# A graph-and-experts network on one core: sums products tied to later gathers in the edge layers, and records of four numbers in the first edge sort

## The chip, the cores and the metric

The kernel runs on one core of a Trainium2 chip. The metric is the device time of one execution in microseconds; lower is better. Five engines of the core matter: TensorE (PE in the profile, with its weight loads PEld), VectorE (DVE), ScalarE (ACT), GpSimd (POOL) and SyncE (SP), and the core's 16 DMA engines.

## The reference, cut to what matters

The network has 3125 nodes of 256 numbers and 53125 edges (src, dst), and four layers, each added to x: an attention over the edges, a mixture of 16 experts, a layer of typed relations over the edges, and a feed-forward of half the tokens.

```python
# layer 0, per head h of 4 (feats = LN(x) @ Ws[h] + bs[h], 64 wide)
score = a_s[:, src] + a_d[:, dst] + aw_e[:, None] * elem[None, :] + ab[:, None]
w = jnp.exp(-jax.nn.relu(score / 20.0))
pooled = segment_sum(w[:, None] * feats[:, dst], src)     # sums over the edges of a node
out = pooled / segment_sum(w, src)[..., None]
...
# layer 2 (called layer 1 of the edges here), h = LN(x)
score = h[src] @ w_src + h[dst] @ w_dst + rel_emb[etype] @ w_rel
alpha = exp(leaky_relu(score)); alpha /= sum(alpha, axis=1)   # one number per edge
msg = (h[src] + rel_emb[etype]) @ weight_neighbor * alpha
node = relu(segment_sum(msg, dst)) + where(in_deg > 0, h @ loop_weight, h @ evolve_loop_weight)
```

The edges are given in the order of dst. Layer 0 sums by src, so its edges are sorted by src in the kernel; layer 1 sums by dst and takes them as they come. `elem` (edge_weight) is float32 and must keep its 32 bits through the sort.

## The kernel before

**Order of the program.** `run` (L2047) goes through: the sort of layer 0's edges with the features of layer 0 between its steps; edge layer 0 (`heads_edges`, L1055) with two fillers, the layout of layer 1's edges and the gate of the experts, which is called for the bucket just finished and has its larger part after every fifth bucket; the experts; the router; edge layer 1 (`relations_edges`, L1621); the last feed-forward (`depths`). A second use of `sort_edges` for layer 1 stands under a branch that is taken only where the edges do not come in order.

**The sort** (`sort_edges`, L297). The edges lie as 128 x 416. `load_in` (L321) packs each into V small numbers that float16 holds exactly (`dig`): the other node's number less an offset, the row in its bucket of 128 nodes (plus 1, so that 0 means an empty place), and, with `bits`, the float32 weight as three pieces of 11, 11 and 10 bits. V is 5 with the weight and 3 without. `places` computes where each edge goes. `move` (L564) runs 13 times, over 32 columns each: for eight columns at a time, DVE compares (`hp`, `hk`) and spreads the records over the places (`hv`, four instructions of 128x400 at L593), and TensorE multiplies the two at L598, adding up in one bank of PSUM. ScalarE copies the result (L606) and GpSimd scatters it with five indirect DMAs (L609) into the table `s_tab` in DRAM, one row of eight records per partition. `load` (L618) reads the table back when all 65 scatters have landed, turns it with TensorE, and unpacks `idx`, `row` and `val` with DVE; `join_bits` (L787) puts the three pieces together. The first gather of edge layer 0 needs `idx`.

**An edge layer.** The edges lie in 25 buckets of 128 nodes, 24 of 18 tiles and one of 8, a tile being 128 edges: 440 tiles. Six tiles are a group; a bucket is three groups. `edge_stages` (L874) gives three stages and `pipelined` (L966) interleaves them: at step s it issues gather(s), message(s-1) and add(s-2), in this order on each engine.

- gather: six indirect DMAs of GpSimd (L907), one per tile, each fetching 128 table rows into one of `deep` buffers `rows` (5 in layer 0, 4 in layer 1); DVE builds the one-hot matrices `oh` (L915) and `hot` (L924).
- message: `near` products of TensorE (L933), reduced by DVE (L940), then `messages`: weights per edge by DVE and ScalarE. In layer 0 the rows are multiplied in place (L1099); in layer 1 ScalarE scales the one-hots (`ohw`, L1645) and the rows get a one-hot of the relation. Before a bucket's second group in layer 1, `loops` (L1650) computes the node's own part into PSUM (L1654), where `finish` of the bucket before must have read its own.
- add: TensorE sums the messages into the bucket's nodes (L953), one float32 product per tile, 260 columns wide in layer 0 and 457 in layer 1; the profile records each as two matmuls. When the bucket's last group is done, DVE adds the overflow (L961) and `finish` follows; in layer 1 that is two transposes at L1666 (`ps_cnt`), two products (`ps_rel`) and DVE's additions into x.

A buffer `rows` is free again when the add of its group is done; so gather(g) waits for add(g - deep). Within TensorE's order in layer 1, the first product of a new bucket stands between the two `ps_cnt` transposes of the bucket before, and its second to fifth before the products at L1654. Each indirect DMA signals one of eight completion semaphores, taken in turn, and a product waits for that of its own tile.

Of the kernel before, what the change touches and what calls it, by code (L numbers as in the profile page):

```python
# [9 lines left out]
F32 = mybir.dt.float32  # L10
BF16 = mybir.dt.bfloat16
F16 = mybir.dt.float16
I32 = mybir.dt.int32
AF = mybir.ActivationFunctionType
OP = mybir.AluOpType
AX = mybir.AxisListType
# [2 lines left out]
P = 128  # L19
# [3 lines left out]
class _Kernel:  # L23
# [8 lines left out]

    def __init__(self, ctx, tc, a, out):
        self.ctx, self.tc, self.nc, self.a, self.out = ctx, tc, tc.nc, a, out
# [259 lines left out]
    def sort_edges(self, pool, rp, name, seg, other, value, bits, tab, help, roomy, into=()):  # L297
# [23 lines left out]
        def load_in():  # L321
            seg_i = tmp(I32, "seg")
            self.load_edges(seg_i, seg, self.NP, nc.vector)
            oth_i = tmp(I32, "oth")
            self.load_edges(oth_i, other, 0, nc.vector)
            val = tmp(F32 if bits else I32, "val")
            self.load_edges(val, value, 0, nc.vector)
            yield
            vi = val.bitcast(I32) if bits else val
            bi = tmp(I32)  # L330
            nc.vector.tensor_scalar(bi, seg_i, 7, None, op0=OP.logical_shift_right)
            bf = tl([P, EC], F32, "bf")
            nc.vector.tensor_copy(bf, bi)
            st.update(bf=bf)
            if roomy:
                st["bt"] = tl([P, C, NS], BF16, "bt")
                nc.vector.tensor_copy(st["bt"], bi.rearrange("p (s t) -> p t s", t=C))


            dig = tl([P, V, EC], F16, "dig", pool)  # L340
            part = tmp(I32)
            nc.vector.tensor_scalar(part, seg_i, P - 1, None, op0=OP.bitwise_and)
            nc.vector.tensor_scalar(dig[:, 1, :], part, 1.0, None, op0=OP.add)
            nc.vector.tensor_scalar(dig[:, 0, :], oth_i, -float(self.half), None, op0=OP.add)
            if bits:
                for i, (sh, m) in enumerate(((0, 2047), (11, 2047), (22, 1023))):
                    v = tmp(I32)
                    nc.vector.tensor_scalar(
                        v, vi, sh, m, op0=OP.logical_shift_right, op1=OP.bitwise_and
                    )  # L350
                    nc.scalar.copy(dig[:, 2 + i, :], v)
            else:
                nc.scalar.copy(dig[:, 2, :], vi)
            st.update(dig=dig)
            yield
# [262 lines left out]
        def load():  # L618
            nb, m = self.KB, MT // self.KB
            if "idx" not in st:  # L620
                st.update(self.lists(name, 1 + (not bits)))
            wide = st["wide"]
            with tc.tile_pool(name=f"{name}_back", bufs=1) as bp:
                tk = bp.tile([P, nb, P, V], F16, name=f"{name}_tk")
                rows = tab[: MT * PT, :].rearrange("(k a) (e v) -> k (a e) v", a=PT, v=V)
                for i in range(nb):

                    queue = nc.gpsimd if roomy else nc.sync
                    ld = queue.dma_start(tk[:m, i], rows[i * m : (i + 1) * m])
                    for s in sent:  # L630
                        tc.add_manual_dep(
                            ld.ins, s.ins.name,
                            mybir.DependencyInfo(
                                mybir.DependencyClass.Sync, mybir.DependencyReason.DATA
                            ),
                            reason="sorted records",
                        )

                def turned(v):
                    pt = self.psum.tile([P, 1024], F16, tag="B", name=f"{name}_pt", bufs=4)  # L640
                    for i in range(nb):
# [11 lines left out]
                nc.vector.tensor_scalar(kept(st["row"]), turned(1), -1.0, None, op0=OP.add)  # L653
                for i, w in enumerate(wide):
                    wb = bp.tile([P, nb, P], BF16, name=f"{name}_wb{i}")
                    nc.vector.tensor_copy(wb[:m], tk[:m, :, :, 1 + i])
                    nc.sync.dma_start(w.rearrange("(i k) p -> k i p", k=m), wb[:m])
                if bits:
                    d = [bp.tile([P, MT], I32, name=f"{name}_d{v}") for v in range(3)]
                    for v in range(3):  # L660
                        nc.vector.tensor_copy(kept(d[v]), turned(2 + v))
                    self.join_bits(st["val"].bitcast(I32), d)
                else:
                    nc.vector.tensor_copy(kept(st["val"]), turned(2))
            return st

# [120 lines left out]
    def join_bits(self, out, d):  # L787
        nc = self.nc
        nc.vector.scalar_tensor_tensor(
            d[0], d[1], 11, d[0], op0=OP.logical_shift_left, op1=OP.bitwise_or  # L790
        )
        nc.vector.scalar_tensor_tensor(
            out, d[2], 22, d[0], op0=OP.logical_shift_left, op1=OP.bitwise_or
        )

# [11 lines left out]
    def edges_beyond(self, name, st, table, width, near, W, message, sums):  # L807
# [10 lines left out]
        with tc.If(more > 0):  # L818
            with tc.tile_pool(name=f"{name}_far", bufs=1) as pool:
# [6 lines left out]
                with tc.For_i(0, more) as k:  # L826
# [7 lines left out]
                    nc.vector.tensor_scalar(row, rec[:, 1:2], -1.0, None, op0=OP.add)  # L834
                    if V == 5:
                        d = tl("d", [3], I32)
                        nc.vector.tensor_copy(d, rec[:, 2:5])
                        self.join_bits(val.bitcast(I32), [d[:, i : i + 1] for i in range(3)])
                    else:
                        nc.vector.tensor_copy(val, rec[:, 2:3])  # L840
                    rows = tl("rows", [width])
                    nc.gpsimd.indirect_dma_start(
# [31 lines left out]
    def edge_stages(  # L874
# [27 lines left out]
        def gather(g, b, k, n, head, last):  # L902
            if head:
                now[b] = [spread(i, b) for i in range(len(st["wide"]))]
            rows = pool.tile([P, G, into], F32, name="rows", bufs=deep)
            for j in range(n):
                self.last_gather = nc.gpsimd.indirect_dma_start(  # L907
                    out=rows[:, j, :width], out_offset=None, in_=table,
                    in_offset=bass.IndirectOffsetOnAxis(
                        ap=st["idx"][:, k + j : k + j + 1], axis=0  # L910
                    ),
                )
            sh = [P, n, P]
            oh = pool.tile([P, G, P], F32, name="oh", bufs=3)
            nc.vector.tensor_tensor(  # L915
                oh[:, :n, :], numbers[:, None, :P].to_broadcast(sh),
                st["row"][:, k : k + n, None].to_broadcast(sh), op=OP.is_equal,
            )
# [29 lines left out]
        def add(g, b, k, n, head, last, oh, msg):  # L948
# [1 line left out]
                now["sum"] = sums2[:, b % 2 * 512 : (b % 2 + 1) * 512]  # L950
            ps = now["sum"]
            for j in range(n):
                nc.tensor.matmul(  # L953
                    ps[:, :W], oh[:, j, :], msg[:, j, :],
                    start=(head and j == 0), stop=(last and j == n - 1),
                )
            if last:
                more = pool.tile([P, W], F32, name="more")
                nc.sync.dma_start(more, sums[b])
                acc = pool.tile([P, W], F32, name="acc")  # L960
                nc.vector.tensor_add(acc, ps[:, :W], more)  # L961
                finish(b, acc)

        return gather, message, add

    def pipelined(self, stages, fill=()):  # L966

# [1079 lines left out]
    def run(self):  # L2047
# [110 lines left out]
```

## Time and profile before

| | us |
|---|---|
| median of 3 runs | 2326.38 (2322.57 to 2326.58) |
| the profiled execution | 2333.29 |
| its span | 2331.5 |
| mean granted clock of TensorE in it | 0.796 |

The stages, by where their instructions stand in the trace:

| stage | from to, us | what runs |
|---|---|---|
| packing, places | 0 to 109 | DVE, ScalarE |
| move and scatters of layer 0 | 109 to 268.5 | DVE, TensorE, 65 scatters |
| load, unpacking | 268.5 to 282 | DMA, DVE |
| edge layer 0 | 282 to 993 | gathers 282 to 968 |
| experts | 1045 to 1376 | TensorE |
| edge layer 1 | 1436 to 2190 | gathers 1436 to 2166 |
| last feed-forward | to 2331 | TensorE, DVE, DMA |

How the profile is read: the page has the busy time of each engine in 40 slices of the span, the groups of instructions by source line (busy time, mean duration of one in ns, and the idle time of the engine just before them with what ended it), and the waits. These are the 40 slices, busy share in tenths, with the clock that TensorE was granted:

```profile
PE   3787244343534544449999964677778777777588
DVE  8999444454444553553222244445556454554731
POOL 1088676656565664413333312455556555555051
PEclk7599666677666776659999987788888888888789
```

A slice is 58 us. The nines in DVE's second to fourth slice are the sort; PE's nines from slice 18 to 22 are the experts; the two long stretches of middling digits are the edge layers.

### The profile page before, as it was taken

How to read it: one execution, taken by the hardware profiler on the slowest of the kernel's cores; microseconds unless marked ns; L12 is line 12 of the kernel's file. 1: busy time of each engine (PE TensorE's matmuls, PEld its weight loads, DVE VectorE, ACT ScalarE, POOL GpSimd, SP SyncE). 2: the span in 40 equal slices, each digit the busy share in tenths (PEclk: the TensorE clock that was granted, in tenths of full speed). 3: DMA queues.
4: the chain of work that ended last, by engine and by line, in shares of the span. 5: the costliest groups of instructions: out<-in, count | busy, mean ns of one | idle time of the engine just before them, and what ended most of it. 6: DMA issues, size and time to landing. Idle time of an engine off the chain costs nothing. (4 is left out here: it accounts for less than half of the span.)

```text
span 2331.5 us, 22343 instructions
## 1 busy us (share of the span) xinstructions
PE 1514.6 (65%) x6602; PEld 940.0 (40%) x6602; DVE 1166.3 (50%) x3010; ACT 424.0 (18%) x1148; POOL 1127.2 (48%) x1133
## 2 busy tenths in 40 slices
PE   3787244343534544449999964677778777777588
PEld 1265133332433433326666643333334333333256
DVE  8999444454444553553222244445556454554731
ACT  1311000100001000102122224122222222222421
POOL 1088676656565664413333312455556555555051
PEclk7599666677666776659999987788888888888789
DMA  3040244443444443249999956444444444443130
GB/s 96 27 158 27 74 115 118 122 114 106 126 117 108 119 129 95 71 137 343 300 316 314 319 192 191 128 128 131 131 130 135 126 131 130 131 130 99 61 121 19
DMA packets 250714, 324.52 MB, mean 139 GB/s; under 512 B 38128, under 2 KB 185008, under 8 KB 250582
## 3 DMA queue, kind: packets, MB, share of 16 engines
q1 hardware_dynamic: 192214, 179.00, 24.6%
q0 software_dynamic: 51760, 137.35, 20.6%
q10 hardware_dynamic: 6608, 6.62, 0.8%
q8 instruction: 57, 0.93, 0.2%
q14 instruction: 75, 0.61, 0.1%
HBM read 286.26 MB, written 36.61 MB: 138 GB/s over the span
## 5 line engine op out<-in xcount | busy, mean ns | idle before, releaser
L907 POOL DMA_INDIRECT rows<-table,s_idx x880 | 836.8, 951 | 590.5 <-issue 291.7
L953 PE MATMUL ps_sums<-rows,oh 128*128 128x260 f32 x880 | 271.6, 474 | 250.0 <-issue 247.0
L953 PE MATMUL ps_sums<-rows,ohw 128*128 128x457 f32 x880 | 395.6, 597 | 13.6 <-issue 11.9
L953 PEld LDWEIGHTS ps_sums<-rows,oh 128*128 128x128 f32 x880 | 206.2, 241 | 302.2 <-issue 258.2
L953 PEld LDWEIGHTS ps_sums<-rows,ohw 128*128 128x128 f32 x880 | 177.4, 209 | 187.6 <-issue 169.7
L915 DVE TENSOR_TENSOR oh<-ps_hold,s_row 128x768 f32<-128x768 f32 (+1 forms) x148 | 139.2, 941 | 139.5 <-remote 103.6
L1387 PE MATMUL ps_h<-w,x_t 128*128 128x512 f32 x448 | 204.5, 599 | 0.0
L924 DVE TENSOR_SCALAR hot<-wide,pcols 128x768 bf16<-128x768 bf16 (+1 forms) x296 | 173.4, 591 | 26.7 <-remote 12.7
L1654 PE MATMUL ps_hold<-lw,x_t 128*128 128x512 f32 x100 | 82.8, 974 | 116.8 <-DVE oh L915 83.0
L1409 POOL DMA_INDIRECT ytab<-y,back x56 | 55.0, 982 | 203.2 <-DVE y L1408 194.3
L1645 ACT ACTIVATE ohw<-oh,s 128x128 f32<-128x128 f32 x440 | 136.3, 388 | 66.7 <-DVE s L1598 33.5
L940 DVE TENSOR_REDUCE near<-ps_near 128x24 f32<-128x72 f32 (+2 forms) x148 | 28.9, 197 | 236.8 <-remote 194.9
L1639 DVE TENSOR_TENSOR rows<-ps_hold,s_val 128x1200 f32<-128x1200 f32 x74 | 102.8, 1389 | 84.5 <-remote 34.2
L609 POOL DMA_INDIRECT s_tab<-s_rec,s_to x65 | 125.5, 1931 | 30.0 <-issue 18.8
L1393 DVE TENSOR_TENSOR hid<-hid,ps_h 128x512 f32<-128x512 f32 x56 | 38.5, 687 | 199.1 <-ACT hid L1392 195.4
L933 PEld LDWEIGHTS <-hot 128*128 128x128 bf16 x1760 | 64.6, 100 | 179.1 <-DVE hot L924 98.2
L1099 DVE TENSOR_TENSOR rows<-rows,ps_hold 128x1536 f32<-128x1536 f32 x74 | 128.0, 1730 | 0.7 <-ACT ps_hold L1097 0.3
L1387 PEld LDWEIGHTS ps_h<-w,x_t 128*128 128x128 f32 x448 | 81.7, 193 | 81.1 <-issue 81.0
L1404 PE MATMUL ps_y<-w,h_t 128*128 128x256 f32 x448 | 105.9, 379 | 0.7 <-ACT h_t L202 0.7
L1097 ACT ACTIVATE ps_hold<-s 128x24 f32<-128x24 f32 x74 | 14.3, 193 | 502.5 <-DVE s L1093 99.1
L961 DVE TENSOR_TENSOR acc<-ps_sums,more 128x260 f32<-128x260 f32 (+1 forms) x50 | 26.5, 529 | 155.9 <-remote 92.9
L593 DVE TENSOR_TENSOR s_hv<-s_hk,s_dig 128x400 f16<-128x400 f16 x208 | 100.6, 677 | 0.0
(410 smaller groups left out, 2057.4 us busy)
## 6 DMA issues: line engine op xcount, KB each, us to landing
w<-in_L_ffn_w_dram SPq DMA_DIRECT2D x168, 512.0 KB
wide<-s_w SPq DMA_DIRECT2D x72, 576.0 KB
rows<-table,s_idx POOLq DMA_INDIRECT x880
sums<-sums_z SPq DMA_DIRECT2D x5, 1142.5 KB
more<-sums SPq DMA_DIRECT2D x25, 228.5 KB
yg<-ytab SPq DMA_DIRECT2D x5, 1024.0 KB
sums<-sums_z SPq DMA_DIRECT2D x5, 650.0 KB
table<-f ACTq DMA_DIRECT2D x5, 650.0 KB
```

Of the source, the lines that this page charges most:

```text
L593: nc.vector.tensor_tensor(rec[:, i], hk[:, i, :, None, :].to_broadcast(sh), dig[:, None, :, t0 + 2 * i : t0 + 2 * i + 2].to_broadcast(sh), ...
L609: d = nc.gpsimd.indirect_dma_start(out=tab, out_offset=bass.IndirectOffsetOnAxis(ap=to[:, i : i + 1], axis=0), in_=out[:, k * CH * V : (k ...
L907: self.last_gather = nc.gpsimd.indirect_dma_start(out=rows[:, j, :width], out_offset=None, in_=table, in_offset=bass.IndirectOffsetOnAxis( ...
L915: nc.vector.tensor_tensor(oh[:, :n, :], numbers[:, None, :P].to_broadcast(sh), st["row"][:, k : k + n, None].to_broadcast(sh), op=OP.is_equal,
L924: nc.vector.tensor_scalar(t[:, : n // 2, :], w, at, None, op0=OP.is_equal)
L953: nc.tensor.matmul(ps[:, :W], oh[:, j, :], msg[:, j, :], start=(head and j == 0), stop=(last and j == n - 1),)
L1099: nc.vector.tensor_tensor(rows[:, :n, :HO].rearrange("p j (h o) -> p j h o", o=O), rows[:, :n, :HO].rearrange("p j (h o) -> p j h o", o=O) ...
L1387: nc.tensor.matmul(ph[:, i * HID : (i + 1) * HID], xt[:, c, :], w12[:, i, c, :], start=(c == 0), stop=(c == C - 1),)
L1404: nc.tensor.matmul(py[:, :D], ht[:, c, :], w3[:, c, :], start=(c == 0), stop=(c == HC - 1))
L1639: nc.vector.tensor_tensor(rows[:, :n, R0:], self.numbers[:, None, :R].to_broadcast(sh), st["val"][:, k : k + n, None].to_broadcast(sh), op ...
L1645: nc.scalar.activation(ow[:, j, :], oh[:, j, :], AF.Copy, scale=s[:, 1, j : j + 1])
L1654: nc.tensor.matmul(self.held_ps[:, : 2 * D], ht[:, c, :], lw[:, c].rearrange("p i d -> p (i d)"), start=(c == 0), stop=(c == C - 1),)
```

## The change

**Waits.** In gather, the six indirect DMAs are kept in a list; in add at the same step, which is two groups behind, each product takes the next of them and gets a dependence on it. Product j of group g thus waits for gather j of group g+2. Nothing else in the stages differs, and the order of instructions on each engine stays as it was. The last two groups have no gather to wait for.

**Records.** With the weight's bits, V is 4 instead of 5. The first number stays. The second holds the row and the weight's low four bits (16 times row plus bits, plus 1), up to 2048. The other 28 bits go as two numbers of 14, each plus 1024, written as the bit pattern of a float16. So `hv` is 128x320, a product of the sort 160 columns, a scattered row 64 bytes and the table a fifth smaller. Packing takes two more DVE operations, a ScalarE cast that also adds the 1 replaces three, and unpacking goes through `split_row` and two subtractions.

```diff
-            nc.vector.tensor_scalar(dig[:, 1, :], part, 1.0, None, op0=OP.add)
             if bits:
-                for i, (sh, m) in enumerate(((0, 2047), (11, 2047), (22, 1023))):
+                low = tmp(I32)
+                nc.vector.tensor_scalar(low, vi, 15, None, op0=OP.bitwise_and)
+                both = tmp(F32)
+                nc.vector.scalar_tensor_tensor(
+                    both, part, 16.0, low, op0=OP.mult, op1=OP.add
+                )
+                nc.scalar.activation(dig[:, 1, :], both, AF.Copy, bias=1.0)
+                for i, sh in enumerate((4, 18)):
                     v = tmp(I32)
                     nc.vector.tensor_scalar(
-                        v, vi, sh, m, op0=OP.logical_shift_right, op1=OP.bitwise_and
-                    )
-                    nc.scalar.copy(dig[:, 2 + i, :], v)
+                        v, vi, sh, 16383, op0=OP.logical_shift_right, op1=OP.bitwise_and
+                    )
+                    nc.vector.tensor_scalar(
+                        dig[:, 2 + i, :].bitcast(I16), v, float(self.LEAST), None, op0=OP.add
+                    )
...
                 if bits:
+                    self.split_row(
+                        bp.tile([P, nb, P], I32, name=f"{name}_wl")[:m],
+                        bp.tile([P, nb, P], I32, name=f"{name}_wh")[:m], tk[:m, :, :, 1],
+                        wb := bp.tile([P, nb, P], BF16, name=f"{name}_wb")[:m], 1.0,
+                    )
+                    nc.sync.dma_start(wide[0].rearrange("(i k) p -> k i p", k=m), wb)
                     d = [bp.tile([P, MT], I32, name=f"{name}_d{v}") for v in range(3)]
-                    for v in range(3):
-                        nc.vector.tensor_copy(kept(d[v]), turned(2 + v))
+                    self.split_row(kept(d[0]), kept(d[1]), turned(1), kept(st["row"]), 0.0)
+                    for v in (1, 2):
+                        nc.vector.tensor_scalar(
+                            kept(d[v]), turned(1 + v).bitcast(I16), float(self.LEAST), 0.0,
+                            op0=OP.subtract, op1=OP.max,
+                        )
                     self.join_bits(st["val"].bitcast(I32), d)
...
+    def split_row(self, low, high, src, row, add):
+        nc = self.nc
+        nc.vector.tensor_scalar(low, src, -1.0, None, op0=OP.add)
+        nc.vector.tensor_scalar(high, low, 4, None, op0=OP.arith_shift_right)
+        nc.vector.tensor_scalar(row, high, add, None, op0=OP.add)
+        nc.vector.tensor_scalar(low, low, 15, None, op0=OP.bitwise_and)
...
             rows = pool.tile([P, G, into], F32, name="rows", bufs=deep)
+            now["came"] = came = []
             for j in range(n):
                 self.last_gather = nc.gpsimd.indirect_dma_start(
...
+                came.append(self.last_gather)
...
             for j in range(n):
-                nc.tensor.matmul(
+                mm = nc.tensor.matmul(
                     ps[:, :W], oh[:, j, :], msg[:, j, :],
                     start=(head and j == 0), stop=(last and j == n - 1),
                 )
+                if now["came"]:
+                    self.behind(mm, now["came"].pop(0), "TensorE in step with the gathers")
...
+    def behind(self, ins, other, reason):
+        self.tc.add_manual_dep(
+            ins.ins, other.ins.name,
+            mybir.DependencyInfo(mybir.DependencyClass.Sync, mybir.DependencyReason.DATA),
+            reason=reason,
+        )
...
-        tab0, tab1 = self.edge_table("s0", 5), self.edge_table("s1", 3)
+        tab0, tab1 = self.edge_table("s0", 4), self.edge_table("s1", 3)
```

More of the change, by code (lines that the diff above doesn't have):

```diff
@@ L13 @@
 I32 = mybir.dt.int32
+I16 = mybir.dt.int16
 AF = mybir.ActivationFunctionType
@@ L23 @@
 class _Kernel:
+    LEAST = 1024
     def __init__(self, ctx, tc, a, out):
@@ L342, in load_in @@
             nc.vector.tensor_scalar(part, seg_i, P - 1, None, op0=OP.bitwise_and)
-            nc.vector.tensor_scalar(dig[:, 1, :], part, 1.0, None, op0=OP.add)
             nc.vector.tensor_scalar(dig[:, 0, :], oth_i, -float(self.half), None, op0=OP.add)
             if bits:
-                for i, (sh, m) in enumerate(((0, 2047), (11, 2047), (22, 1023))):
+                low = tmp(I32)
[6 more added lines that the diff above has]
+                for i, sh in enumerate((4, 18)):
                     v = tmp(I32)
                     nc.vector.tensor_scalar(
-                        v, vi, sh, m, op0=OP.logical_shift_right, op1=OP.bitwise_and
+                        v, vi, sh, 16383, op0=OP.logical_shift_right, op1=OP.bitwise_and
                     )
-                    nc.scalar.copy(dig[:, 2 + i, :], v)
+                    nc.vector.tensor_scalar(
+                        dig[:, 2 + i, :].bitcast(I16), v, float(self.LEAST), None, op0=OP.add
+                    )
             else:
+                nc.vector.tensor_scalar(dig[:, 1, :], part, 1.0, None, op0=OP.add)
                 nc.scalar.copy(dig[:, 2, :], vi)
@@ L652, in load @@
                 )
[L653 to L657, printed above, removed]
-                if bits:
-                    d = [bp.tile([P, MT], I32, name=f"{name}_d{v}") for v in range(3)]
-                    for v in range(3):
-                        nc.vector.tensor_copy(kept(d[v]), turned(2 + v))
+                if bits:
+                    self.split_row(
[4 more added lines that the diff above has]
+                    nc.sync.dma_start(wide[0].rearrange("(i k) p -> k i p", k=m), wb)
+                    d = [bp.tile([P, MT], I32, name=f"{name}_d{v}") for v in range(3)]
+                    self.split_row(kept(d[0]), kept(d[1]), turned(1), kept(st["row"]), 0.0)
[4 more added lines that the diff above has]
+                        )
                     self.join_bits(st["val"].bitcast(I32), d)
                 else:
+                    nc.vector.tensor_scalar(kept(st["row"]), turned(1), -1.0, None, op0=OP.add)
+                    for i, w in enumerate(wide):
+                        wb = bp.tile([P, nb, P], BF16, name=f"{name}_wb{i}")
+                        nc.vector.tensor_copy(wb[:m], tk[:m, :, :, 1 + i])
+                        nc.sync.dma_start(w.rearrange("(i k) p -> k i p", k=m), wb[:m])
                     nc.vector.tensor_copy(kept(st["val"]), turned(2))
@@ L789, in join_bits @@
         nc.vector.scalar_tensor_tensor(
-            d[0], d[1], 11, d[0], op0=OP.logical_shift_left, op1=OP.bitwise_or
+            d[0], d[1], 4, d[0], op0=OP.logical_shift_left, op1=OP.bitwise_or
         )
         nc.vector.scalar_tensor_tensor(
-            out, d[2], 22, d[0], op0=OP.logical_shift_left, op1=OP.bitwise_or
+            out, d[2], 18, d[0], op0=OP.logical_shift_left, op1=OP.bitwise_or
         )
+    def split_row(self, low, high, src, row, add):
[4 more added lines that the diff above has]
+        nc.vector.tensor_scalar(low, low, 15, None, op0=OP.bitwise_and)
     def parts(self, dst, src, tmp):
@@ L833, in edges_beyond @@
                     nc.vector.tensor_scalar(idx, rec[:, 0:1], float(self.half), None, op0=OP.add)
[L834 to L838, printed above, removed]
+                    if V == 4:
+                        d = [tl(f"d{i}", [1], I32) for i in range(3)]
+                        self.split_row(d[0], d[1], rec[:, 1:2], row, 0.0)
+                        for i in (1, 2):
+                            nc.vector.tensor_scalar(
+                                d[i], rec[:, 1 + i : 2 + i].bitcast(I16), float(self.LEAST), 0.0,
+                                op0=OP.subtract, op1=OP.max,
+                            )
+                        self.join_bits(val.bitcast(I32), d)
                     else:
+                        nc.vector.tensor_scalar(row, rec[:, 1:2], -1.0, None, op0=OP.add)
                         nc.vector.tensor_copy(val, rec[:, 2:3])
```

## The prediction

> **What bounds the kernel now.** I read the page by stretches first, since five stages with different limits follow one another, then cut the span into the stretches that the change touches, then the waits of POOL, and last the gathers one by one. In the cut below each row gives start:end and width, the busy time of PE, PEld, DVE, ACT and POOL with instruction counts, the granted clock, the DMA share and GB/s.
>
> ```profile
> 50.00:100.00 50.00, 32.35 (x37) 9.51 (x38) 49.79 (x120) 19.40 (x21) 0.00 (x0) 0.50 0.01 1
> 120.00:240.00 120.00, 96.89 (x555) 72.15 (x553) 120.00 (x279) 20.96 (x58) 105.09 (x46) 0.96 0.25 81
> 282.00:968.00 686.00, 297.48 (x1380) 233.92 (x1381) 320.81 (x757) 50.37 (x175) 420.94 (x444) 0.69 0.42 116
> 1436.00:2166.00 730.00, 526.07 (x2440) 260.61 (x2441) 366.33 (x936) 168.69 (x568) 415.47 (x440) 0.82 0.46 131
> ```
>
> To be seen: from 120 to 240 us, while the edges of layer 0 are sorted, DVE has no gap at all. In the edge layers (rows 3 and 4) no engine is full: the 440 gathers keep POOL busy for 421 and 415 us of 686 and 730, and TensorE runs at a clock of 0.69 and 0.82.
>
> ```profile
> L907 POOL DMA_INDIRECT rows<-table,s_idx x880 | 836.8, 951 | 590.5 <-issue 291.7
> L953 PE MATMUL ps_sums<-rows,oh 128*128 128x260 f32 x880 | 271.6, 474 | 250.0 <-issue 247.0
> L953 PE MATMUL ps_sums<-rows,ohw 128*128 128x457 f32 x880 | 395.6, 597 | 13.6 <-issue 11.9
> L609 POOL DMA_INDIRECT s_tab<-s_rec,s_to x65 | 125.5, 1931 | 30.0 <-issue 18.8
> L593 DVE TENSOR_TENSOR s_hv<-s_hk,s_dig 128x400 f16<-128x400 f16 x208 | 100.6, 677 | 0.0
> ```
>
> A gather takes 0.95 us of POOL and the next starts 0.30 us later: 440 x 1.25 = 550 us is the floor of a layer. What lies above it (136 and 180 us) is POOL standing before the first gather of a group. The waits say for what:
>
> ```profile
> POOL rows L907 <- PE ps_sums L953: 195.0, 37, 18.2
> PE ps_hold L1654 <- DVE oh L915: 83.0, 14, 8.6
> DVE near L940 <- remote: 194.9, 32, 16.4
> ```
>
> Row 1: 195 us in 37 waits, until TensorE has done the sums that free the rows buffer. In layer 1 (132 us of the 195) such a wait ends 0.27 us after the sums of the group four back. Those come late because the bucket's products at L1654 wait for DVE, which has finish of the bucket before to do first (row 2). In layer 0 the 63 us are mostly four waits of 13 to 18 us, at every fifth bucket, where the gate's work is added; another 19 stalls of about 3.5 us, one per bucket, come while a TensorE signal reaches the others 3 to 12 us after the product's record has ended (row 3, "remote"). The trace does not say why.
>
> **Part 1, records of four numbers.** *The sort of layer 0.* L593 becomes 128x320 instead of 128x400, 208 times. The recorded 677 ns overlaps with its neighbours; start to start, four of them and the two comparisons before them repeat every 2.60 us, 0.417 us for each L593. Scaled by elements, 0.333 us: 208 x 0.083 = 17 us of DVE. DVE is full in this stage, so nothing of its own hides that. But the end of the stage is POOL: 65 scatters at L609, one per DVE iteration while DVE runs (2.33 us busy, 2.63 from start to start), and 1.26 us each once DVE is done at 245.6 us. Some 18 remain then and take 23 us, to 268.5:
>
> ```profile
> DVE o_seg L707 <- DMA s_tab<-s_rec,s_to: 22.5, 1, 22.5
> ```
>
> If scatters remain tied to DVE's iterations (each ends about 1.05 us after a comparison starts), the same 47 are done when DVE ends, 17 us earlier, and all 17 pass through. If they stay at 2.63 us, 17 us less of DVE leaves 6.5 more scatters for the tail at 1.26 us: 8 us return, 9 are gained. The starts follow DVE closely, so I take 16. Scatters of 64 bytes a row instead of 80 I cost at nothing: the tail's 0.96 us is the same as a gather's 0.95 with over a kilobyte a row, so it isn't bytes. TensorE's products shrink too (200 to 160 columns), and at 96.9 of 120 us it does not stop DVE.
>
> *Before it.* In the packing DVE gets two more operations of 128x416 at about 0.5 us: +1 us, uncovered, since DVE is busy 49.8 of 50 us there. ScalarE goes from three casts to one, hidden.
>
> *After it.* Five more DVE operations unpack the row and the bits before the first gather, which stands 9.9 us behind DVE there: about +1.5 us; the load is a fifth smaller and one transpose round less goes: −0.5. Sum of part 1: −16 + 1 + 1 = **−14 us**, ends −6 and −20 (28 by the recorded 677 ns would be the extreme, which the pitch excludes).
>
> **Part 2, each sums product waits for a gather.** No instruction is added: the product already waited for its own group's gather and now waits for the one two groups, 12 tiles, on, which was issued at the same step. TensorE executes in order: behind a waiting product stand the rest of the group's sums, the next near products, and in layer 1 the transposes, the x_t and the L1654 of a bucket's end. DVE (near, acc), ScalarE and finally POOL's buffers wait for those.
>
> I set the last packet of every gather (median 2.4 us after its issue) against the start of the product that shall wait for it.
>
> *Layer 0*: the gather has landed 9.4 us before in the median group; in 15% of the groups it is late, by at most about 3 us, and those groups free their buffer 15 to 20 us before POOL asks. Cost 0 likely; 3 us x 11 groups = 33 as the upper end if the cover were gone.
>
> *Layer 1*: the median lead is only 2 us and 36% of the groups would wait. Mostly it is a group's last product by 0.5 to 1.2 us, at 3 to 6 us of slack. The place that matters is a bucket's first product: in TensorE's order it stands between the two ps_cnt transposes of the bucket before, and in every second bucket its gather lands 2.5 to 2.7 us too late (the products at 1584.5 and 1643.0 us, for instance). Twelve such places x 2.6 = 31 us if all is on the chain; 0 if the slack of these groups, 2.0 to 2.7 us, covers it. Nothing is late next but L1654, whose wait (row 2 above) takes up part.
>
> *Below nothing*: spreading the products evenly also has a gain side. TensorE's bursts alternate with cold stretches, and the 19 stalls of 3.5 us in layer 0 (67 us) hang on signals that come late behind a burst; if an even stream ends them, they go. So part 2 lies between −67 and +64; with no way of reading in this trace whether the signals mend, I take 0.
>
> *A rule against this change.* The row first: from 50 to 100 us evenly spaced float32 products, 65% busy, stayed at a clock of 0.50 for the whole stretch. The Trainium skill, "TensorE: Matmul & The Clock Gate", Part 1 (HAM oscillation), says that a wait for a DMA between groups of products lets the array throttle to half speed again. By the rule, layer 1 could fall to 0.50 throughout: 526 us x 0.82 / 0.50 = 863 us of TensorE in a stage of 730, +133 us. By the rows, layer 1 is 72% busy at 0.82, more than that stretch; a sums product needs 0.77 us of the 1.25 between gathers when warm and 1.52 when cold, so a cold TensorE would have no gaps left and warm up. I follow the rows: 0. In layer 0 a cold product (0.87 us) fits in 1.25, so a cold clock costs there 6 x 0.42 = 2.5 us of delay per group against 8 us of median slack: hidden.
>
> **The sum.** −14 + 0. The profiled execution's span of 2331.5 us becomes 2317; with the 1.8 us around it, 2333.3 becomes 2319. The shown runs' median, 2326.4, is 6.9 below the profiled one: **2312 us**.
>
> **Rivals.**
> - *The bucket's first product holds up the bucket's end* (slower): the 31 us at the second ps_cnt transpose, less 14: 2326 + 17 = **2343**. It decides from a wait of about 2.7 us on, the slack of those groups. For: 27 buffer waits in layer 1 already end 0.27 us after the sums. Against: the products at L1654 stand on another wait anyway.
> - *An even stream mends the late signals and cold spells*: of the 67 us in layer 0 some 40 go, **2272**. For: the stalls come once a bucket, beside a burst. Against: the cause isn't seen.
> - *The scatters, not DVE, set the sort*: gain 9 − 2, less a little for waits of layer 1: about **2323**. For: POOL 105 of 120 us busy. Against: scatter ends follow the comparisons, and the tail runs at 0.96 us.
> - *TensorE goes cold in layer 1*: half of the 133 us, less 14: **2379**.
>
> **How the numbers follow.** Forecast 0.42 (own range 2300 to 2326), late bucket's end 0.25, mended signals 0.18, scatters 0.10, cold 0.05. What this measurement can tell from no change is 0.2%, 4.7 us: faster is below 2321.7, slower above 2331.0. Faster: nearly all of the forecast (0.37), the mended signals (0.18) and some of the scatters' case (0.03), 0.58; slower: most of the late end (0.23) and the cold case, 0.28; the same 0.14. The range 2265 to 2352 leaves out the cold case, the long end of the mended signals and the worst of the late ends, some 2 in 10.
>
> **What would show it.** L593 near 0.33 us apart and DVE's part of the sort ending 16 us earlier, the first gather near 268 us instead of 282. The tail wait at L707 still near 22 us if scatters follow DVE, near 30 if not. In layer 1, sums that wait for a rows DMA, and the buffer waits above or below 132 us; in layer 0 whether the 3.5 us stalls remain. The prediction is wrong if the two edge stages change by more than 15 us either way, or if the clock in either falls.

## The result, and the profile after

The changed kernel takes 2396.7 us (2384.7 to 2401.3, 4 runs) beside 2324.5 (2321.2 to 2326.6) for the kernel before: a ratio of 1.029, interval 1.026 to 1.033. It is slower, where faster was forecast, and outside the range of 2265 to 2352. Its profiled execution has a span of 2383.0 us against 2331.5.

The kernel before itself takes 2324 us in this comparison and in one set of the experiments and 2011 us in the other three sets; differences are therefore taken only within a set, and the last section says what differs.

Where the 51.5 us of the two spans lie, by the first and last gathers of each trace:

| stretch | before, us | after, us | difference |
|---|---|---|---|
| start to first gather (sort of layer 0) | 282.2 | 266.9 | −15.3 |
| gathers of layer 0 | 687.4 | 683.0 | −4.4 |
| to the first gather of layer 1 | 466.6 | 465.2 | −1.4 |
| gathers of layer 1 | 730.3 | 804.7 | +74.4 |
| to the end | 164.9 | 163.3 | −1.6 |

Two executions of the kernel before under the same conditions differ by 21 us in the gathers of layer 1 (730 here, 709 in experiment 9), so the rows of a few us say little; the 74 stand clear of that (the changed kernel's second trace, experiment 8, has 809 us).

The cut of the changed kernel's span into stretches, in the columns shown before the prediction (start:end and width, busy time of PE, PEld, DVE, ACT, POOL, the granted clock, DMA share, GB/s):

```profile
119.00:233.00 114.00, 91.02 (x577) 70.25 (x576) 111.90 (x291) 21.32 (x60) 98.35 (x51) 0.96 0.27 91
267.00:950.00 683.00, 314.37 (x1387) 237.70 (x1388) 325.26 (x766) 50.88 (x176) 424.21 (x445) 0.68 0.42 117
1415.00:2220.00 805.00, 590.92 (x2442) 288.24 (x2443) 366.91 (x937) 168.85 (x568) 417.51 (x440) 0.76 0.42 119
```

To be seen: layer 0 is as it was; in layer 1 POOL, DVE and ScalarE have the same busy time in 75 us more, only TensorE's has grown (526 to 591 us), and its clock has fallen from 0.82 to 0.76. The groups of instructions on the changed kernel's page:

```profile
L993 PE MATMUL ps_sums<-rows,ohw 128*128 128x457 f32 x880 | 436.7, 643 | 68.6 <-DMA rows<-table,s_idx 53.8
...
L624 POOL DMA_INDIRECT s_tab<-s_rec,s_to x65 | 111.1, 1710 | 28.9 <-issue 18.8
```

The sums of layer 1 now have 68.6 us of idle time before them instead of 13.6, most of it ended by a gather's DMA: the new wait. The scatters of the sort became shorter (1931 to 1710 ns mean). And the waits of PE and POOL in layer 1 of the changed kernel (what waited, what for, total us, times, longest):

```profile
PE ps_hold L1704 <- DVE oh L955: 91.3, 21, 7.3
PE ps_sums L993 <- DMA rows<-table,s_idx: 53.8, 33, 3.4
```

```profile
POOL rows L946 <- PE ps_sums L993: 194.4, 41, 17.1
POOL rows L946 <- issue: 117.3, 382, 1.2
POOL rows L946 <- DVE rows L1689: 71.3, 7, 10.4
```

The added waits are 54 us in all. POOL's waits for a free buffer were 132.3 us in the same stretch before; now they are 194.4, and 71.3 more with another name at their end; those seven too end 0.27 us after the sums of the group four back, as the trace's times show. So TensorE waits for POOL and POOL waits longer for TensorE.

**One bucket of layer 1.** The mean of buckets 4 to 23 (A, B, C are its three groups, A' the first group of the next bucket; the bucket of A' is counted), from the products' times in the traces; "records" and "layer 1" are the first and third experiment below, taken where the kernel before runs in 2011 us:

| step of TensorE, us | before | after | records | layer 1 |
|---|---|---|---|---|
| end of A to end of B's sums | 8.3 | 5.6 | 5.6 | 5.6 |
| to end of C's sums | 4.6 | 5.9 | 4.8 | 5.2 |
| to the first product of A' | 0.9 | 3.1 | 0.9 | 2.4 |
| that product | 0.9 | 1.8 | 0.9 | 1.4 |
| to the second (ps_cnt, ps_rel, near, x_t between) | 1.7 | 2.6 | 1.7 | 2.5 |
| second to fifth | 3.2 | 5.1 | 3.2 | 4.2 |
| to the products at L1654 | 5.2 | 4.1 | 1.7 | −0.2 |
| to the end of A' | 4.6 | 4.9 | 3.5 | 2.6 |
| sum: a bucket | 29.5 | 33.1 | 22.5 | 23.7 |

(−0.2: the first of these products starts before the recorded end of the fifth; the ends of matmuls are modelled.)

Between before and after, C's sums and the first product of A' wait 3.4 us longer, the products from there to the fifth take 3.6 us longer, at a colder clock, and B's sums and L1654 give 3.8 back. A bucket's 18 gathers need 22.5 us of POOL.

### The profile page after: what moved, and what is told of

Same layout as the page of the kernel before. It is cut to its first block, busy times and chain, and to the rows that moved or that the text cites. A ratio compares the mean times of both kernels' runs of the same rounds, so it can differ in the third digit from the quotient of the medians.

```text
span 2383.0 us, 22336 instructions
## 1 busy us (share of the span) xinstructions
PE 1577.2 (66%) x6598; PEld 960.9 (40%) x6598; DVE 1154.8 (48%) x3017; ACT 423.5 (18%) x1146; POOL 1116.4 (47%) x1133
## 5 line engine op out<-in xcount | busy, mean ns | idle before, releaser
L993 PE MATMUL ps_sums<-rows,ohw 128*128 128x457 f32 x880 | 436.7, 643 | 68.6 <-DMA rows<-table,s_idx 53.8
L993 PE MATMUL ps_sums<-rows,oh 128*128 128x260 f32 x880 | 285.6, 486 | 251.7 <-issue 157.1
L993 PEld LDWEIGHTS ps_sums<-rows,ohw 128*128 128x128 f32 x880 | 187.7, 224 | 262.5 <-issue 232.3
L1704 PE MATMUL ps_hold<-lw,x_t 128*128 128x512 f32 x100 | 88.2, 1032 | 94.3 <-DVE oh L955 91.3
L624 POOL DMA_INDIRECT s_tab<-s_rec,s_to x65 | 111.1, 1710 | 28.9 <-issue 18.8
L1454 PEld LDWEIGHTS ps_y<-w,h_t 128*128 128x128 f32 x448 | 85.0, 190 | 36.0 <-issue 26.3
```

The source lines that it names most:

```text
L624: d = nc.gpsimd.indirect_dma_start(out=tab, out_offset=bass.IndirectOffsetOnAxis(ap=to[:, i : i + 1], axis=0), in_=out[:, k * CH * V : (k ...
L993: mm = nc.tensor.matmul(ps[:, :W], oh[:, j, :], msg[:, j, :], start=(head and j == 0), stop=(last and j == n - 1),)
L1454: nc.tensor.matmul(py[:, :D], ht[:, c, :], w3[:, c, :], start=(c == 0), stop=(c == HC - 1))
L1704: nc.tensor.matmul(self.held_ps[:, : 2 * D], ht[:, c, :], lw[:, c].rearrange("p i d -> p (i d)"), start=(c == 0), stop=(c == C - 1),)
```

## The experiments

All edits are of the changed kernel, and its lines are meant. Where an expectation gives a time for conditions in which the kernel before takes 2324 us and the run fell where it takes 2011, or the other way round, only the difference to the kernel before or to the records alone can be held against it.

**1. Records of four without waits.**

```diff
-                if now["came"]:
-                    self.behind(mm, now["came"].pop(0), "TensorE in step with the gathers")
```

> The records of four numbers without any wait on a later gather. Theory (the loss comes from the waits in layer 1 alone): the first gather 15 us earlier, both edge layers as before, 2324 - 16 = 2308 us. Rival (the shorter records have a price elsewhere, for instance in the edge layers by other addresses or a later unpacking): above 2316.

1993.4 us against 2010.9: 0.991, interval 0.990 to 0.993, −17.5. The first gather starts at 267.0 us. The gain of the records is there, alone. Its two edge layers:

```profile
267.00:822.00 555.00, 322.67 (x1439) 249.03 (x1440) 331.67 (x788) 53.91 (x185) 421.52 (x445) 0.74 0.53 145
1272.00:1827.00 555.00, 477.20 (x2449) 238.00 (x2449) 372.08 (x950) 168.50 (x568) 416.61 (x440) 0.94 0.61 173
```

Both stand at the 550 us that 440 gathers need one after another, with TensorE at 0.94 in layer 1. Here POOL is the bound, and any wait that it gets is a loss at once.

**2 and 3. The waits in one layer only.** The condition becomes `if now["came"] and into == W and deep == 5` (layer 0) or `... and deep == 4` (layer 1).

> Records of four, waits in layer 0 only. Theory: in layer 0 the waits are covered by the 9 us of median release slack, gathers of layer 0 again take 683 us against 687 before: 2303 to 2309. Rival (a part of the loss sits in layer 0 and was hidden by chance in the profiled run): 2320 or more.

2000.8 us: 0.995 of the kernel before (0.993 to 0.997), and 7.4 more than the records alone. The gathers of layer 0 take 555 us in both; the price comes behind them. The last sums end 14.0 us after the last gather in this trace, 9.4 in that of experiment 1, and the first gather of layer 1 comes 6 us later after it. The three other traces with these waits in the same conditions have 14.6 to 15.7 us there, the three without them 9.4 to 10.8. So the waits of layer 0 were not quite free, as the theory had it, and cost less than the 12 us or more of its rival.

> Records of four, waits in layer 1 only. Theory: all of the loss is here, 33 us a bucket instead of 29.5: 2385 to 2400, as the whole change. Rival (half of it is from layer 0's waits): 2345 to 2365.

2026.1 us: 1.008 (1.006 to 1.010), 33 more than the records alone: most of the loss is here, as the theory had it, though at less than half of its size, which was for the other conditions. The gathers of layer 1 take 587 us instead of 554:

```profile
1272.00:1858.00 586.00, 512.49 (x2448) 258.77 (x2449) 367.46 (x945) 169.11 (x568) 416.12 (x440) 0.87 0.58 163
```

What PE and POOL waited for in this stretch, and for comparison POOL with the records alone (third line):

```profile
PE ps_sums L993 <- DMA rows<-table,s_idx: 35.6, 25, 3.1
POOL rows L946 <- PE ps_sums L993: 49.0, 45, 5.5
POOL rows L946 <- PE ps_sums L993: 7.3, 11, 4.3
```

This trace shows the cause in one bucket. First TensorE (near products left out), then POOL's three gathers that count, from the timeline (start us, duration, line, count, and the idle time before it with what ended it):

```profile
1546.74 0.93 PE L993 MATMUL ps_sums<-rows,ohw 128*128 128x457 f32 x2
...
1558.90 0.33 PE L1716 MATMUL ps_cnt<-ident,acc 128*128 128x128 f32 x1 [0.73 <-DVE acc L1003]
1560.69 1.01 PE L993 MATMUL ps_sums<-rows,ohw 128*128 128x457 f32 x2 [1.46 <-DMA rows<-table,s_idx]
1561.53 0.27 PE L1716 MATMUL ps_cnt<-ident,acc 128*72 128x128 f32 x1
...
1564.16 5.49 PE L993 MATMUL ps_sums<-rows,ohw 128*128 128x457 f32 x8
1569.49 1.88 PE L1704 MATMUL ps_hold<-lw,x_t 128*128 128x512 f32 x4
1571.20 0.93 PE L993 MATMUL ps_sums<-rows,ohw 128*128 128x457 f32 x2
```

```profile
1547.94 0.94 POOL L946 DMA_INDIRECT rows<-table,s_idx  x1 [1.05 <-PE ps_sums L993]
...
1555.42 0.94 POOL L946 DMA_INDIRECT rows<-table,s_idx  x1 [0.30 <-PE ps_sums L993]
...
1572.41 0.94 POOL L946 DMA_INDIRECT rows<-table,s_idx  x1 [2.28 <-PE ps_sums L993]
```

The last product of A ends at 1547.67 and frees a buffer; 0.27 us later POOL starts the six gathers of the group four on. Six gathers on, at 1555.42, comes the first gather of the group five on, and that is the one for which the first product of A' waits (A' is three groups on, plus two). That product runs at 1560.69; the bucket's end, four cold products (5.5 us) and L1704 follow; the last product of A' ends at 1572.13, and only then does POOL get its next buffer, 2 us late. The loop from buffer to buffer is 1572.41 − 1547.94 = 24.5 us, and POOL needs 22.5. **Sums wait for gathers and gathers for sums, in one closed loop.**

Two things make the loop long in each bucket. One is how late the awaited gather lands. It is issued at 1555.42 and its last signal comes at 1560.55, 5.1 us later; over buckets 4 to 23 gathers at this place land 5.2 us after their issue (median), the twelve before them in the bucket 2.8 to 2.9. At 1555.35 SP issues the two loads of `wide` for the next bucket, 576 KB each, and the DMA engines are full until the awaited gather has landed. After SP's line from the timeline, three stretches in the columns of the cut above; the last three columns are clock, DMA share and GB/s:

```profile
1555.35 1.54 SPq L935 DMA_DIRECT2D wide<-s_w  x2
1548.00:1556.00 8.00, 8.00 (x41) 4.05 (x39) 8.00 (x20) 2.51 (x9) 6.18 (x7) 1.00 0.35 93
1556.00:1561.00 5.00, 2.81 (x8) 1.11 (x7) 1.21 (x4) 2.13 (x7) 3.78 (x5) 1.00 0.97 271
1562.00:1568.00 6.00, 6.00 (x30) 3.35 (x29) 4.58 (x16) 0.68 (x3) 4.48 (x6) 0.50 0.55 162
```

The other is the clock, which is 0.50 from 1562 to 1568: in the table the steps from the first product of A' to the fifth take 2.3 us more than with the records alone. The mean bucket is only 1.2 us above POOL's 22.5. As an estimate from these figures, either the 2.4 us of late landing or the 2.3 us of cold products, if taken away, would bring the loop below that; no run here takes away one of them alone, so how the loss divides between them is not shown.

**4 and 5. Which product closes it.** In experiment 4 every product but the first of a bucket waits in layer 1 (`if not (head and j == 0 and deep == 4)` ahead of the wait); in experiment 5 only that one does (`if deep == 5 or (head and j == 0)`).

> The whole change, but in layer 1 the first product of a bucket, the one between the two ps_cnt transposes, keeps its old wait. Theory of the loop (sums wait for the gather two groups on, that gather waits for a buffer which the sums four groups before it free, so gathers and sums take turns): the wait of that product, 2.2 us a bucket, moves to the next products and TensorE is still cold, so most of the loss stays: 2365 or more. Rival (that one place holds the end of the bucket, as the prediction's rival had it): back to 2303 to 2320.

> The whole change, but in layer 1 only the first product of a bucket waits for the gather two groups on; the others keep their old wait. Theory of the loop: this one wait closes it (the sums of the bucket's first group free the buffer of the group before the one that is waited for), so most of layer 1's cost stays: 2365 to 2395 where the kernel before takes 2324, 2018 to 2030 where it takes 2011. Rival (the cost is a sum over all waiting products): a third or less of it, 2335 or less, and 2010 or less.

2029.1 us (1.009, interval 1.007 to 1.010) and 2029.3 (1.009, 1.008 to 1.011). The figure given for the first was for the other set of conditions; the second lies in the range of its theory. Both are 18 us above the kernel before, where all waits together are 26 above it (experiment 10): either half of layer 1's waits costs most of what the whole costs. The gathers of layer 1 take 583 and 585 us, against 587 with all waits. Without the first product's wait, C's sums take 6.9 us a bucket instead of 4.8: the last product of C waits for the gather just ahead. The waits do not add; either half closes the same loop.

**6 and 7. Opening the loop**, in the set where the kernel before takes 2324.6 us. In one, each product waits for the gather of the next group instead of the next but one; in the other, layer 1 has five buffers.

```diff
+            now["prev"] = now.get("came")
             now["came"] = came = []
...
-                if now["came"]:
-                    self.behind(mm, now["came"].pop(0), "TensorE in step with the gathers")
+                if now.get("prev") is not None and j < len(now["prev"]):
+                    self.behind(mm, now["prev"][j], "TensorE in step with the gathers")
```

> Each product waits for the gather of the group one further on instead of two. Theory of the loop: the gather it waits for is issued 7.5 us earlier, so the loop from the sums of a group over the gather that takes its buffer back to the sums is shorter by 7.5 us and no longer above the 22.5 us of a bucket's gathers: within 4 us of the records alone (1993 where the kernel before takes 2011). Rival (a wait on a gather costs TensorE's clock at any distance): above 2010 there.

2311.9 us, 0.995 (0.992 to 0.998), 12.7 less than the kernel before. The rival's loss did not come. The theory's "within 4 us of the records alone" can't be held against this: the records alone were not run in these conditions.

```diff
-                early=loops, deep=4,
+                early=loops, deep=5,
```

(and `w2` allocated and loaded in `depths`, `agg` and `ct` with one buffer)

> The whole change with five rows buffers in layer 1 instead of four; to make room, one matrix of the last layer is loaded after the edge layer and two tiles of finish have one buffer. Theory of the loop: the sums of a group now release the gather five on, which is the very one the next bucket's first product waits for; the loop is 0.3 + 3 + 0.5 + 11.4 = 15 us against 22.5 and the cost of layer 1's waits goes: 1997 to 2005 where the kernel before takes 2011 (layer 0's 7 us stay). Rival (the waits cost by the cold clock and by their place in TensorE's order, whatever the buffers): 2025 to 2035.

2313.0 us, 0.996 (0.993 to 0.998), 11.6 less. All waits of the change are in it, two groups on, and the loss is gone; its rival is out, the theory's range was for the other conditions. The stretch behind the gathers is 9 us longer than in experiment 6, but that is not the later load: the gathers are one group further ahead of the sums (the last sums end 29.6 us after the last gather, 20.1 there), and what follows the sums takes 143 us in both. Layer 1 of experiments 6 and 7, in the columns of the cut above:

```profile
1415.00:2146.00 731.00, 529.79 (x2441) 261.33 (x2442) 366.54 (x941) 168.85 (x568) 415.98 (x440) 0.83 0.46 131
1420.00:2132.00 712.00, 518.40 (x2393) 255.30 (x2394) 359.46 (x923) 165.97 (x560) 416.09 (x440) 0.83 0.47 133
```

The time is that of the kernel before (730 and 709 us) and the clock too (0.82). PE's waits in layer 1 of experiment 7:

```profile
PE ps_hold L1704 <- DVE oh L955: 58.2, 13, 8.6
PE ps_hold L1704 <- ACT x_t L206: 30.7, 6, 6.4
PE ps_near L973 <- DVE hot L964: 24.1, 5, 20.4
```

No wait of the sums for a gather is among the longest any more. With five buffers the sums of A release the very gather for which A' waits, and six gathers (7.5 us) drop out of the loop. Both edits also free the loop of the late landing: the gather that is awaited now lands 2.5 us after its issue (median of buckets 4 to 23). What five buffers would give in these conditions without any wait was not measured, so only experiment 6 compares waits with waits alone.

**8 to 10. The kernels themselves.**

> The whole change, beside the kernel before on the chip that runs the parts. If this chip is one where the kernel before takes 2011 us: theory (parts add: records -17.5, waits of layer 0 +7, waits of layer 1 +33) 2011 + 22 = 2033, the profile without late TensorE signals (x_t read by ScalarE 0.2 us after its product). If it is one where it takes 2324: 2397 again. Rival (the two waits disturb each other): 2050 or more on the first kind of chip.

2397.6 us against 2324.6 in the set of experiments 6 and 7: 1.032 (1.027 to 1.037), the first result again, with 809 us of gathers in layer 1. The loss that those two remove is 73 plus 12 us.

> The kernel before, for its trace on the chip that runs the experiments. Theory (what differs between 2324 and 2011 us is how late TensorE's signals reach the other engines, not the program): edge layers at the floor of 550 us of gathers each, sort stage as in the first trace, x_t read by ScalarE within 0.3 us of its product. Rival (a different clock alone): the signals are late here too, and the layers above 600 us.

2310.5 us in its one run, in the same set: layer 1 709 us, x_t read 6.9 us after the next product has begun. The expectation was for the other conditions; the run says nothing on what makes them.

> The whole change again, to have it beside its parts where the kernel before takes 2011 us. Theory: records -16, layer 0's waits +7, layer 1's +32 (the same loop whichever of its products wait): 2034 there, its layer 1 at 585 us from first to last gather. Rival (late signals, not the loop, made the loss in the first comparison): 2010 or less there. Where the kernel before takes 2324, 2397 as before, which tells nothing new.

2036.7 us against 2011.1: 1.013 (1.011 to 1.014), +26 where the parts give −16 + 7 + 33 = +24, and 588 us of gathers in layer 1. The loss is there without late signals too, at less than half the size.

**11 and 12. Without the waits, with four buffers and with five.** The records alone once more, and with five buffers in layer 1 (as in experiment 7, with the load of `w2` moved to ScalarE's queue behind the gathers of `depths`).

> Records of four numbers without waits once more, for its ratio on whichever chip this is. Theory (the gain is 16 us of the sort's DVE time, in full): 2308 where the kernel before takes 2324, 1994 where it takes 2011. Rival (on the slower chip the gain is lost in the edge layers): 2318 or more there.

1995.7 us, 0.993 (0.991 to 0.994) of 2011.2.

> Records of four, no waits, five rows buffers in layer 1; one matrix of the last layer is loaded after the edge layer and two tiles of finish have one buffer. A version that may beat both kernels. Theory (where TensorE's signals are late, POOL stands in layer 1 for the sums of the group four back; one more buffer lets it run 7.5 us further): 2280 to 2300 where the kernel before takes 2324, and 1993 to 1998, no gain over the records alone, where it takes 2011 and the gathers run without a gap. Rival (the bucket's end sets the pace in either case): 2308 on the slower chip too.

1996.8 us, 0.993 (0.992 to 0.994): no gain over the records alone, where the gathers have no gaps. Whether it gains where the kernel before takes 2324 us was not measured, as this set fell in the other conditions. Where the kernel before takes 2011 us, the records alone beat both kernels, by 15 to 18 us and by 41.

## Why the prediction failed

**Part 1 was right.** Forecast −14 with ends −6 and −20; the first gather comes 15.3 us earlier, and experiments 1 and 11 give −17.5 and −15.5. One reading was off without harm to the sum: DVE's last L593 of the sort ends at 247.5 us in the trace of before, not at 245.6. L593's instruction is now 0.342 us from the next (forecast 0.333, before 0.415); DVE's last one starts 14.6 us earlier. The choice that the scatters follow DVE held: their period went from 2.635 to 2.345 us as one of DVE's iterations did (2.629 to 2.339), and the wait for the table is 20.9 us after 22.5, not 30.

**Layer 0** was forecast at 0 with an upper end of 33. In the first traces it is even (−4); measured alone the waits cost 7 us, not at the buffers, whose slack covered them as forecast, but mostly at the drain of the pipeline behind the last gather, a place that the prediction did not look at.

**Layer 1 is the step that failed**: "Twelve such places x 2.6 = 31 us if all is on the chain; 0 if the slack of these groups, 2.0 to 2.7 us, covers it", of which 0 was taken; measured are 33 us in experiment 3 and 74 in the first traces. The prediction's own sign of being wrong, an edge stage off by more than 15 us or a falling clock, came true. The place was right: the product between the two ps_cnt transposes. What failed is the overlap that it counted on, and the method behind it. Leads and slacks were read from the trace of before and taken as fixed while a wait was put in. But the gather that the product waits for is itself released by sums four groups back, so the wait moves the gather on, and the next wait with it. In the trace of before, buckets of about 24 and 36 us alternated, and in every second one the gather had landed in time or was late by less than 1 us; those were counted as free. After, nearly every bucket waits (2.2 us more ahead of the first product, on the mean). A stage with such a loop is priced by its length against the bound, here 24.5 against 22.5 us in the bucket shown, 23.7 in the mean, and then times the number of buckets: 25 x 1.2 = 30 us, near the 32 by which experiment 3's gathers take longer. (This is worked out afterwards, from the same trace.) Where the signals of TensorE are late, the bucket's end is longer: 33.1 us against 29.5 in the mean of those twenty buckets, and 74 us in all. There the kernel before does not run at POOL's 22.5 either, so that size was not worked out; experiments 6 and 7 show that it hangs on the same loop.

**The rival "the bucket's first product holds up the bucket's end"** named the mechanism and the side, and was the one to follow: 2343 with 31 us. Its size was short for the same reason; that experiment 3's 33 us lie so near its 31 is chance, for the 31 were twelve waits in the conditions in which 74 were lost. That it decides from a wait of 2.7 us on was wrong: what decides is the length of the loop against the 22.5 us of POOL, not one wait against one slack. Nor is that product alone the cause (experiment 4).

**The clock.** The rule of the Trainium skill ("TensorE: Matmul & The Clock Gate", Part 1, HAM oscillation) is for DMA waits between groups of products that leave TensorE idle for more than about 3.4 us, after which the next group starts at half speed. It was set aside for the rows, at 0 us against 133. Neither was right. The clock of layer 1 fell from 0.82 to 0.76, and from 0.94 to 0.87 between experiments 1 and 3. In experiment 3's trace the gap ahead of a bucket's first product is 2.5 us (median, 0.3 of it a transpose), shorter than in the rule, and still the clock falls to 0.50 within 3.5 us of that product's start in 18 of the 20 buckets, mostly for 3.4 or 6.8 us. The products after the wait run cold, second to fifth in 5.1 us instead of 3.2 after the change. The longer steps at a cold clock are half of those in the table, and they lie in the loop. It does not stay cold throughout: that part of the prediction's argument held. What the argument missed is that the mean busy share says nothing of the ten microseconds right after a wait. How much the cold clock alone costs was not measured by itself.

**The gain side** ("mended signals") did not come: the late signals are as late after as before (x_t 7.2 and 7.1 us after the second product's start, on the mean).

## What to carry to other kernels

Before a wait is added between two engines, follow the awaited instruction back to what releases it; if that leads to the waiting engine, the two make a loop, and its length per turn against the bound's time per turn is the price, whatever slack a trace without the wait shows. Look for the number of buffers in that loop: with one more the loss was gone here, and so it was with waiting one group less far ahead. Look also at what else the DMA engines carry when the awaited transfer runs: here it landed 2.4 us late in the median bucket beside two loads. Taking out some of several waits in the same loop gains little, so an experiment on a single one of them can mislead.

## What the runs showed of the hardware that was not expected

The same kernel took 2324 us in some sets and 2011 in others. In the traces of the first kind TensorE's signals reach other engines late, once a bucket; the waits of the changed kernel in the first comparison:

```profile
ACT x_t L206 <- remote: 238.3, 28, 10.0
DVE near L980 <- remote: 229.6, 32, 16.6
```

In the trace of the records alone, of the second kind, no wait ends this way, and x_t is read 0.2 us after the next product starts. Durations of gathers (0.95 us), scatters (2.03 us at the median) and DVE's instructions are the same in both kinds. SP's 245 register moves, 29 ns at the median in both, take 15 to 21 us together in the traces of the first kind and 7 in those of the second. What brings the late signals about stays open: no run here was made to tell it, and they came and went between sets of the same program, on one and the same chip too (that of experiments 6 to 9 ran 5, 11 and 12 some six minutes later without them).
